# A sparse graph network on one core: gathered rows in a ring, VectorE's order written out, the stages of a group moved closer

## The chip, the cores and the metric

The kernel runs on one core of one Trainium2 chip. Its time is the device time of one execution in microseconds; less is better. The core has five engines with an instruction queue each: TensorE (PE; its weight loads are listed apart as PEld), VectorE (DVE), ScalarE (ACT), GpSimd (POOL) and SyncE (SP, which only starts transfers here). DMA engines move the data; a transfer is started from the queue of SP, ScalarE or GpSimd.

## The reference

Four layers work on 3327 nodes with 256 values each. Layers 0, 2 and 3 are the same block of attention and feed-forward with their own weights, layer 1 is an averaging layer. A node attends only to its neighbours in `adj` (0.24% of all pairs, and itself):

```python
def block(x, adj, w_qkv, w_proj, b_proj, w1, b1, w2, b2, g1, be1, g2, be2):    # 8 heads of 32
    q, k, v = split(layer_norm(x, g1, be1) @ w_qkv)
    scores = jnp.where(adj != 0, einsum('nhd,mhd->hnm', q, k) * SCALE, -inf)
    out = einsum('hnm,mhd->nhd', softmax(scores), v).reshape(n, DIM)
    x = x + out @ w_proj + b_proj
    return x + gelu(layer_norm(x, g2, be2) @ w1 + b1) @ w2 + b2                # 256 -> 1024 -> 256

def averaging(x, adj, Wt, bt, Wa, ba, Wp, bp, gamma, beta):
    h = x @ Wt.T + bt                                                          # 64 values
    s = leaky_relu(h @ Wa.T + ba)                                              # one score a node
    tf = softmax(where(adj > 0, s, NEG), axis=1) @ h @ Wp.T + bp
    return layer_norm(x + tf) * gamma + beta

x = block(x, adj, ...); x = averaging(x, adj, ...); x = block(x, adj, ...); x = block(x, adj, ...)
```

(Abridged: `split` takes the three parts of each row apart.)

## The kernel before

Nodes are handled in 26 tiles of 128 (NP = 3328). The program has five stages, one after the other: adjacency, block 0, averaging, block 1, block 2. The adjacency stage loads the matrix, finds each node's neighbours and sorts the nodes by how many they have; from then on tile 0 holds the nodes with most neighbours. `ROOM[t]` is the number of neighbours, without the node itself, that tile t has places for:

```python
ROOM = [24, 14, 12, 12, 11, 11, 10, 10, 9, 9, 9, 9, 8, 8, 8, 7, 7, 7, 7, 6, 6, 6, 5, 5, 4, 4]
```

They add up to 228; with each node's own row 254 a block.

A block goes through its tiles in the order of `GROUPS` (from few neighbours to many), in groups of one to four tiles. For a tile, `scores` (from line 552) does the following.

- GpSimd starts one indirect DMA for each neighbour place (`gather`, line 546): 128 rows of keys and values, 512 numbers each, into a buffer `unit` of four such places. Ten buffers go round. The node's own row (`own`: key, value, query, x) comes by an indirect DMA (block 0) or from SP's queue (lines 564, 566).
- ScalarE copies x out of `own` (line 568, blocks 0 and 1) and the query into a PSUM bank `qs` (line 571; two banks go round; it also holds the tile's scores).
- VectorE multiplies keys by the query and adds up each head (`dot`: lines 576 and 577), once for `own` and once for each unit of four rows; then it adds the mask (591), takes the maximum (593) and subtracts it (595). ScalarE takes the exponential (596).

`weighed` (from line 599) is done one step after a tile's `scores`: VectorE adds up the exponentials (605), divides (606, 607), multiplies values by weights (610, again once for `own` and once for each unit) and adds: unit upon unit (622, 626), then a unit's four rows in two steps (630), then onto `own`'s part in `o` (631).

When all tiles of a group have their `o`, `project` transposes them (658), copies the transposes (659, ScalarE) and multiplies by the projection's weights (664), after a small matmul that puts the bias into PSUM (`bias`, line 189). The remaining stages of a group are put into a list `later` with the step at which they are to be issued, and `run` issues what is due after each tile: stage 0 is `feed_forward` (VectorE adds the projection onto x at 671, ScalarE sums the squares at 214, VectorE works out the norm in lines 215 to 218, then `turned` normalizes and transposes at 251 to 262, then matmuls f1 at 685, Gelu on ScalarE at 688, matmuls f2 at 695); stage 1 is `end` (the second addition at 671, and what the next layer needs: `finish` of `into_averages` or `into_keys`); stage 2 is the scatter of the results. Stage 0 is due one step after the projection (two for groups of more than two tiles), stage 1 `max(2, len(group))` steps after stage 0.

The order on each engine is not the program's: a scheduler places the instructions of all engines, and VectorE's too, by their dependencies, so that two tiles' work can be mixed. Only the end of the adjacency stage has VectorE's order fixed (`manual_schedule`, line 367). Between a block and the next stage there is a full exchange: the rows that the next layer gathers must have been scattered.

The averaging stage reads a table `between` (its narrow half as `parts`, in two loads at lines 861 to 869), runs `checks` and a column sum (`cps`, `cws`), and then goes through chunks of four tiles: `sums` transposes slices of the stored adjacency on load, into buffers of the same pool as the gathered rows (`units`), and multiplies; a second part makes the averages and block 1's keys.

A dense network stands behind the sparse one, and runs only where the sparse one finds that a node has too many neighbours; in these runs it isn't executed.

## Time and profile before

| | us |
|---|---|
| device time, median of 3 runs | 2089.86 |
| lowest, highest | 2078.97, 2097.79 |
| the profiled execution, its own time | 2096.42 |
| its span in the profile | 2094.6 |
| adjacency / block 0 / averaging / block 1 / block 2 | to 306 / 848 / 1066 / 1604 / the end |

The mean clock granted to TensorE was 0.77 of full speed in the profiled execution. All other times in this document are of such an execution unless they are called a median.

How the profile is read: a row names a line of the kernel, an engine, an operation, the tile written, the tile read, and their shapes, with the number of instructions behind an x; behind the bar the busy time of the group in microseconds, the mean of one in nanoseconds, and the engine's idle time just ahead of them with what ended it. A view by stretches gives each engine's busy time (overlaps of an engine's own instructions counted once) between two moments. A view of waits gives, for an engine and a line, what it waited for: the total in microseconds, how many times, and the longest. A timeline lists single instructions with their start and their duration in microseconds.

### The profile page before, as it was taken

How to read it: one execution, taken by the hardware profiler on the slowest of the kernel's cores; microseconds unless marked ns; L12 is line 12 of the kernel's file. 1: busy time of each engine (PE TensorE's matmuls, PEld its weight loads, DVE VectorE, ACT ScalarE, POOL GpSimd, SP SyncE). 2: the span in 40 equal slices, each digit the busy share in tenths (PEclk: the TensorE clock that was granted, in tenths of full speed). 3: DMA queues.
4: the chain of work that ended last, by engine and by line, in shares of the span. 5: the costliest groups of instructions: out<-in, count | busy, mean ns of one | idle time of the engine just before them, and what ended most of it. 6: DMA issues, size and time to landing. Idle time of an engine off the chain costs nothing. (4 is left out here: it accounts for less than half of the span.)

```text
span 2094.6 us, 17222 instructions
## 1 busy us (share of the span) xinstructions
PE 1263.4 (60%) x4806; PEld 812.1 (39%) x4806; DVE 1342.0 (64%) x3407; ACT 684.9 (33%) x1420; POOL 1001.0 (48%) x946
## 2 busy tenths in 40 slices
PE   3244411556755579699934688567695277655676
PEld 1122200344424337577512454343473154323445
DVE  3567635577776785165636789776732679976871
ACT  3555501233321224122322444334343133322232
POOL 3768757555555531101156645555203666565521
PEclk8667655677767769799976888798798587767778
DMA  8878827555555550858486656656215665565520
GB/s 191 330 300 326 284 79 213 160 163 154 170 148 175 147 131 23 198 154 230 160 284 205 216 166 209 220 178 193 61 56 201 210 186 176 176 190 160 152 65 20
DMA packets 169409, 369.73 MB, mean 177 GB/s; under 512 B 78821, under 2 KB 90291, under 8 KB 165976
## 3 DMA queue, kind: packets, MB, share of 16 engines
q0 software_dynamic: 68624, 222.01, 35.4%
q1 hardware_dynamic: 85689, 112.44, 17.1%
q10 hardware_dynamic: 14990, 34.08, 5.0%
q8 instruction: 40, 0.66, 0.1%
q14 instruction: 66, 0.54, 0.1%
HBM read 279.77 MB, written 77.59 MB: 171 GB/s over the span
## 5 line engine op out<-in xcount | busy, mean ns | idle before, releaser
L546 POOL DMA_INDIRECT unit<-kv,ids x684 | 667.2, 975 | 434.7 <-issue 189.1
L685 PE MATMUL f<-hT,w 128*128 128x256 f32 (+3 forms) x960 | 342.1, 517 | 58.6 <-ACT gT L688 23.2
L256 PE MATMUL tr<-ident,xh 128*128 128x128 f32 x312 | 80.6, 384 | 442.7 <-ACT xh L251 395.6
L695 PE MATMUL f<-w,gT 128*128 128x256 f32 x1248 | 306.4, 399 | 17.9 <-ACT gT L688 14.3
L685 PEld LDWEIGHTS f<-hT,w 128*128 128x128 f32 x960 | 190.4, 219 | 202.6 <-issue 106.0
L695 PEld LDWEIGHTS f<-w,gT 128*128 128x128 f32 x1248 | 238.3, 197 | 68.7 <-ACT gT L688 18.3
L256 PEld LDWEIGHTS tr<-ident,xh 128*128 128x128 f32 x312 | 41.7, 179 | 483.3 <-ACT xh L251 414.8
L576 DVE TENSOR_TENSOR unit<-unit,qs 128x1024 f32<-128x1024 f32 (+3 forms) x198 | 211.7, 1069 | 26.4 <-DMA unit<-kv,ids 15.0
L577 DVE TENSOR_REDUCE qs<-unit 128x32 f32<-128x1024 f32 (+3 forms) x198 | 212.7, 1074 | 4.8 <-DVE qs L607 1.7
L610 DVE TENSOR_TENSOR unit<-unit,qs 128x1024 f32<-128x1024 f32 (+3 forms) x198 | 210.0, 1065 | 0.0
L315 POOL TENSOR_TENSOR m<-a,place 128x3328 f16<-128x3328 fp8e4 x26 | 159.4, 6132 | 78.7 <-ACT a L313 78.6
L688 ACT ACTIVATE gT<-f,b 128x256 f32<-128x256 f32 (+3 forms) x240 | 124.8, 536 | 212.5 <-PE f L685 106.6
L538 PE MATMUL kvps<-wqkv,hT 128*128 128x512 f32 x312 | 171.9, 677 | 29.5 <-ACT hT L262 22.5
L326 DVE MAX8 found<-m 128x8 f16<-128x416 f16 x208 | 111.5, 579 | 39.7 <-POOL m L315 33.1
L664 PE MATMUL proj<-wproj,oT 128*128 128x256 f32 x312 | 109.3, 489 | 42.7 <-ACT oT L659 22.8
L576 DVE TENSOR_TENSOR own<-own,qs 128x256 f32<-128x256 f32 x78 | 32.3, 415 | 141.5 <-ACT qs L571 124.2
L658 PE MATMUL otr<-ident,o 128*128 128x128 f32 x156 | 25.5, 289 | 142.4 <-DVE qs L577 87.4
L990 POOL DMA_INDIRECT sorted<-st,to x26 | 24.8, 955 | 178.7 <-ACT st L542 147.1
L538 PEld LDWEIGHTS kvps<-wqkv,hT 128*128 128x128 f32 x312 | 63.2, 213 | 86.7 <-issue 37.7
L313 ACT ACTIVATE a<-a 128x3328 fp8e4<-128x3328 int32 x26 | 77.3, 2973 | 51.6 <-DMA kv<-st 29.0
L251 ACT ACTIVATE xh<-x,shift,rstd 128x256 f32<-128x256 f32 x104 | 58.4, 594 | 104.5 <-DVE shift L218 80.9
L664 PEld LDWEIGHTS proj<-wproj,oT 128*128 128x128 f32 x312 | 66.9, 235 | 65.6 <-ACT oT L659 28.4
(193 smaller groups left out, 1881.4 us busy)
## 6 DMA issues: line engine op xcount, KB each, us to landing
a<-in_adj SPq DMA_DIRECT2D x25, 1663.5 KB
kv<-st ACTq DMA_DIRECT2D x52, 512.0 KB
own<-sorted SPq DMA_DIRECT2D x26, 512.0 KB
unit<-kv,ids POOLq DMA_INDIRECT x684
adj<-a SPq DMA_DIRECT2D x26, 416.0 KB
own<-qkv SPq DMA_DIRECT2D x26, 384.0 KB
own<-own SPq DMA_DIRECT2D x26, 384.0 KB
w<-in_L_gnn_w SPq DMA_DIRECT2D x6, 1024.0 KB
```

The lines of the kernel that those rows point to most:

```text
L256: nc.tensor.transpose(ps[k][:, ts(q, P)], t[:, ts(k, P)], self.ident)
L315: nc.gpsimd.tensor_mul(m.rearrange("p (s e) -> p s e", e=SEG), a8.rearrange("p (s e) -> p s e", e=SEG), place.unsqueeze(1).to_broadcast([P ...
L326: nc.vector.max(found[:, i, s, :], m[:, ts(s, SEG)])
L538: nc.tensor.matmul(kv, hT[:, k, ts(q, P)], w[:, k, DIM : 3 * DIM], start=k == 0, stop=k == KC - 1)
L546: g = self.nc.gpsimd.indirect_dma_start(out=out, out_offset=None, in_=table, in_offset=bass.IndirectOffsetOnAxis(ap=self.ids[:, t, j : j + ...
L576: nc.vector.tensor_mul(k, k, query.unsqueeze(1).to_broadcast([P, n, DIM]))
L577: nc.vector.tensor_reduce(s[:, ds(at, n), :].rearrange("p j h -> p (j h)"), k.rearrange("p j (h d) -> p j h d", d=HD), AX.X, ALU.add,)
L610: nc.vector.tensor_mul(to.rearrange("p j (h d) -> p j h d", d=HD), v.rearrange("p j (h d) -> p j h d", d=HD), s[:, ds(at, n), :].unsqueeze ...
L664: nc.tensor.matmul(y, oT[:, k, ts(q, P)], wpj[:, k, :], start=False, stop=k == KC - 1)
L685: nc.tensor.matmul(y[:, :w], w1[:, k, ts(f, P)], hT[:, k, :w], start=k == 0, stop=k == KC - 1)
L688: nc.scalar.activation(gT[-1][:, f % 2, :w], y[:, :w], AF.Gelu_apprx_tanh, bias=b1[:, f : f + 1])
L695: nc.tensor.matmul(y, gT[f // 2][:, f % 2, ts(q, P)], w2[:, f, :], start=False, stop=f == FC - 1)
```

## The change

The buffers of four rows are replaced by one ring of 46 places of 512 numbers (`RING`, `take`). A tile takes ROOM + 2 places that lie side by side: its neighbours, and two for its own row, whose key and value then come right behind the neighbours'. So multiplications run over up to six rows at once (`PIECE`, `pieces`), the weighting over up to nine (`WEIGHED`), own row included, and the additions fold the tile's rows in halves.

`fetch` is taken out of `scores`: it starts the own row's and the neighbours' transfers and copies the query, and is called one step ahead, right after `weighed`. x comes by a transfer on SP's queue (block 0: from the ring; block 1: from `sorted`) instead of a copy on ScalarE.

VectorE's instructions in a block keep the order in which the program writes them (`manual_schedule` around the loop); the other engines are scheduled as before. The written order of a step is: `scores` of a tile, the norms and what follows them for groups whose squares are ready (`between`), `weighed` of the tile before, then what `run` has due: additions, squares on ScalarE, scatters. For this `norm` is cut in two (`squares` and `norm`), and `feed_forward` is entered with the squares made. Stage 0 is due one step after the projection, and the second addition `BEHIND` steps after the feed-forward: 2, 2, 3, 3 for groups of one to four tiles. `finish` of `into_averages` hands back its VectorE work (`rest`) to be issued a step later.

The last groups are cut smaller: (6, 5, 4), (3, 2), (1,), (0,) become (6, 5), (4, 3), (2,), (1,), (0,). The last group's feed-forward is put ahead of the other stages that are still due at the end.

A PSUM bank that holds two tiles' results takes both biases in one matmul (`Halves`, `bias`). Gelu results are packed closer into their buffers (`gT`). In the averaging, `parts` is loaded in six pieces in place of two, `checks` and the column sums come after the first chunk's `sums`, and the buffers are places of the ring, each kind by turns.

Of the removed lines only single ones are shown; the longer stretches stand in the kernel above.

```diff
...
+RING = 46
+PIECE = 6
+WEIGHED = 9
...
-    (25, 24), (23, 22), (21, 20, 19), (18, 17, 16, 15), (14, 13, 12, 11), (10, 9, 8, 7), (6, 5, 4), (3, 2), (1,), (0,),
+    (25, 24), (23, 22), (21, 20, 19), (18, 17, 16, 15), (14, 13, 12, 11), (10, 9, 8, 7), (6, 5), (4, 3), (2,), (1,), (0,),
 ]
+BEHIND = (0, 2, 2, 3, 3)
...
+class Halves(list):
+    def __init__(self, banks, n):
+        super().__init__(banks[q // 2][:, ds(q % 2 * DIM, DIM)] for q in range(n))
+        self.banks = banks
+    def bank(self, q):
+        return self.banks[q // 2], min(2, len(self) - q)
+    def ends(self, q):
+        return q % 2 == 1 or q == len(self) - 1
...
-        self.nc.tensor.matmul(y, self.ones3, self.biases[:, i, :], start=True, stop=False)
+    def bias(self, ys, q, i):
+        if q % 2 == 0:
+            bank, n = ys.bank(q)
+            self.nc.tensor.matmul(
+                bank[:, : n * DIM], self.ones3, self.biases[:, i, :].unsqueeze(1).to_broadcast([3, n, DIM]),
+                start=True, stop=False,
+            )
...
             nc.scalar.activation(xh, t, AF.Square, bias=m[:, i : i + 1], accum_out=v[:, i : i + 1])
+        return m, v
+    def norm(self, pool, n, m, v):
+        nc = self.nc
         nc.vector.tensor_scalar(v[:, :n], v[:, :n], 1.0 / DIM, EPS, ALU.mult, ALU.add)
         y = self.root(pool, v, n)
...
+    def take(self, n):
+        if self.at + n > RING:
+            self.at = 0
+        at = self.at
+        self.at += n
+        return self.ring[:, at : at + n, :]
...
-    def scores(self, pool, pp, layer, t, held):
+    def fetch(self, pp, layer, t, held):
         nc = self.nc
         J = ROOM[t]
-        own = pool.tile([P, 4 * DIM], F32, tag="own", name="own", bufs=3)
+        rows = self.take(J + 2)
+        own = rows[:, J:, :].rearrange("p a b -> p (a b)")
         if layer == 0:
             nc.gpsimd.indirect_dma_start(
                 out=own, out_offset=None, in_=self.kv[0][:],
                 in_offset=bass.IndirectOffsetOnAxis(ap=self.row[t], axis=0),
             )
+            nc.sync.dma_start(out=self.x[t], in_=own[:, 3 * DIM :])
         elif layer == 1:
-            self.after(nc.sync.dma_start(out=own, in_=self.sorted[ts(t, P), :]), self.turning)
+            for to, at in ((own[:, : 3 * DIM], self.sorted[ts(t, P), : 3 * DIM]), (self.x[t], self.sorted[ts(t, P), 3 * DIM :])):
+                self.after(nc.sync.dma_start(out=to, in_=at), self.turning)
         else:
             nc.sync.dma_start(out=own[:, : 3 * DIM], in_=self.own[t])
...
+        for j in range(J):
+            self.gather(rows[:, j, :], self.places[layer], t, j, held)
         bank = pp.tile([P, CW], F32, tag="qs", name="qs", bufs=2)
         query = bank[:, :DIM]
         nc.scalar.copy(query, own[:, 2 * DIM : 3 * DIM])
+        return rows, bank
+    def scores(self, pool, t, rows, bank):
+        nc = self.nc
+        J = ROOM[t]
+        n = J + 1
+        query = bank[:, :DIM]
         s = bank[:, ds(DIM, (SLOTS + 1) * HEADS)].rearrange("p (j h) -> p j h", h=HEADS)
...
+        for lo, w in self.pieces(n, PIECE):
+            k = rows[:, ds(lo, w), :DIM]
+            nc.vector.tensor_mul(k, k, query.unsqueeze(1).to_broadcast([P, w, DIM]))
             nc.vector.tensor_reduce(
-                s[:, ds(at, n), :].rearrange("p j h -> p (j h)"), k.rearrange("p j (h d) -> p j h d", d=HD), AX.X,
+                s[:, ds(lo, w), :].rearrange("p j h -> p (j h)"), k.rearrange("p j (h d) -> p j h d", d=HD), AX.X,
                 ALU.add,
             )
...
         away = self.away[:, t, :J].unsqueeze(2).to_broadcast([P, J, HEADS])
-        nc.vector.tensor_add(s[:, ds(1, J), :], s[:, ds(1, J), :], away)
+        nc.vector.tensor_add(s[:, :J, :], s[:, :J, :], away)
         top = pool.tile([P, HEADS], F32, tag="top", name="top", bufs=3)
...
+        nc.vector.tensor_reduce(top, s[:, :n, :].rearrange("p j h -> p h j"), AX.X, ALU.max)
+        nc.vector.tensor_sub(s[:, :n, :], s[:, :n, :], top.unsqueeze(1).to_broadcast([P, n, HEADS]))
+        nc.scalar.activation(s[:, :n, :], s[:, :n, :], AF.Exp)
+        return rows, s
+    @staticmethod
+    def pieces(n, most):
+        count = -(-n // most)
+        at = 0
+        for k in range(count):
+            w = (n - at) // (count - k)
+            yield at, w
+            at += w
+    def weighed(self, pool, t, rows, s):
+        nc = self.nc
+        n = ROOM[t] + 1
         total = pool.tile([P, HEADS], F32, tag="total", name="total", bufs=3)
-        nc.vector.tensor_reduce(total, s[:, : J + 1, :].rearrange("p j h -> p h j"), AX.X, ALU.add)
+        nc.vector.tensor_reduce(total, s[:, :n, :].rearrange("p j h -> p h j"), AX.X, ALU.add)
         nc.vector.reciprocal(total, total)
...
+        nc.vector.tensor_mul(s[:, :n, :], s[:, :n, :], total.unsqueeze(1).to_broadcast([P, n, HEADS]))
+        for lo, w in self.pieces(n, WEIGHED):
+            v = rows[:, ds(lo, w), DIM:].rearrange("p j (h d) -> p j h d", d=HD)
+            nc.vector.tensor_mul(v, v, s[:, ds(lo, w), :].unsqueeze(3).to_broadcast([P, w, HEADS, HD]))
         o = pool.tile([P, DIM], F32, tag="o", name="o", bufs=5)
...
+        v = rows[:, :, DIM:]
         while n > 1:
...
+            half = -(-n // 2)
+            to = v[:, : n - half, :] if n > 2 else o.unsqueeze(1)
+            nc.vector.tensor_add(to, v[:, : n - half, :], v[:, half:n, :])
+            n = half
         return o
...
                     for k in range(KC):
-                        nc.tensor.matmul(y, oT[:, k, ts(q, P)], wpj[:, k, :], start=False, stop=k == KC - 1)
+                        nc.tensor.matmul(
+                            y, oT[:, k, ts(q, P)], wpj[:, k, :], start=False, stop=k == KC - 1 and ys.ends(q)
+                        )
                 return ys
...
-            def feed_forward(group, ys):
+            def squares(group, ys):
+                return self.squares(pool, [self.x[t] for t in group], add(group, ys))
+            def feed_forward(group, sums):
                 w = len(group) * P
-                hT = self.turned(pool, pp, [self.x[t] for t in group], g, b, sums=add(group, ys))
+                hT = self.turned(pool, pp, [self.x[t] for t in group], g, b, sums=sums)
                 gT = []
+                each = 2 * CW // w
                 for f in range(FC):
...
+                    if f % each == 0:
+                        room = pool.tile([P, 2 * CW], F32, tag="gT", name="gT", bufs=4)
+                        gT += [room[:, ds(k * w, w)] for k in range(each)]
...
-            later = []
+            later, middle = [], []
+            def add_later(at, stage, group, what):
+                later.append((at, stage, group, what))
+                later.sort(key=lambda x: (x[0], -x[1]))
+            def forward(at, group, sums):
+                add_later(at + BEHIND[len(group)], 1, group, feed_forward(group, sums))
+                if ahead and group == GROUPS[-1]:
+                    ahead()
+            def follow(at, group, sums):
+                after, rest = finish(group, sums)
+                if rest:
+                    add_later(at + 1, 2, group, rest)
+                add_later(at + 1 + (len(group) > 2 or rest is not None), 3, group, after)
             def run(now):
                 while later and (now is None or later[0][0] <= now):
-                    at, stage, group, ys = later.pop(0)
+                    at, stage, group, what = later.pop(0)
                     if stage == 0:
...
+                        middle.append((forward, at, group, squares(group, what)))
                     elif stage == 1:
-                        later.append((at + 1 + (len(group) > 2), 2, group, end(group, ys)))
+                        if not finish:
+                            add(group, what)
+                            add_later(at + 1 + (len(group) > 2), 3, group, None)
+                        elif normed:
+                            middle.append((follow, at, group, squares(group, what)))
+                        else:
+                            add(group, what)
+                            middle.append((follow, at, group, None))
+                    elif stage == 2:
+                        what()
                     else:
...
+                        scatter(group, what)
+                    if now is None:
+                        between()
+            def between():
+                while middle:
+                    f, *rest = middle.pop(0)
+                    f(*rest)
+            tiles = iter([t for group in GROUPS for t in group])
+            def fetch():
+                t = next(tiles, None)
+                return t is not None and self.fetch(pp, layer, t, held)
+            with tc.manual_schedule(engines={nc.vector.engine}):
+                waiting, step, outs = None, 0, []
+                got = fetch()
+                for group in [*GROUPS, ()]:
+                    for t in group or (None,):
+                        now = t is not None and (group, t, *self.scores(pool, t, *got))
+                        between()
+                        if t is None:
+                            run(step)
+                        if waiting:
+                            done, *rest = waiting
+                            outs.append(attended(*rest))
+                        got = fetch()
+                        if waiting and len(outs) == len(done):
+                            ys, outs = project(done, outs), []
+                            if t is not None:
+                                add_later(step + 1, 0, done, ys)
+                        waiting = now
+                        if begin and step == 2:
+                            begin()
+                        if t is not None:
+                            run(step)
+                        step += 1
+                middle.append((forward, step, done, squares(done, ys)))
+                middle.sort(key=lambda x: x[0] is not forward)
+                between()
+                run(None)
...
+            for lo, hi in ((0, 3), (3, 8), (8, NT // 2)):
+                for n in range(2):
...
+            turn, place = cycle(range(0, 20, 4)), cycle(range(20, 44, 4))
...
-                    at = self.units.tile([P, NT // 2, HALF], BF, tag="unit", name="at")
+                    at = self.ring[:, ds(next(turn), 4), :].rearrange("p a b -> p (a b)").bitcast(BF)[:, : NT // 2 * HALF]
+                    at = at.rearrange("p (g i) -> p g i", i=HALF)
...
+            self.checks(wp, pp, adj)
...
         self.held = []
-        with tc.tile_pool(name="units", bufs=UNITS) as self.units:
+        with tc.tile_pool(name="gathered", bufs=1) as pool:
+            self.ring, self.at = pool.tile([P, RING, 2 * DIM], F32, name="ring"), 0
             self.block(0, got[0], self.into_averages(*args(1, "Wt bt Wa")), lambda: fetch(2, 2))
```

`checks` and the column sums (`cps`, `cws`) move down unchanged. `into_keys` returns `True` as its fourth value (its `finish` is entered with squares), `into_averages` `False`.

## Prediction

> **What bounds the kernel now.** I read the page first (busy shares, chain), then the windows by stage, the waits of VectorE and of GpSimd, and last the timeline of VectorE alone.
>
> ```profile
> PE 1263.4 (60%) x4806; PEld 812.1 (39%) x4806; DVE 1342.0 (64%) x3407; ACT 684.9 (33%) x1420; POOL 1001.0 (48%) x946
> ```
>
> No engine is full; VectorE (DVE) is the fullest. The windows cut the run at its stages: block 0 (306 to 848), averaging (848 to 1066), block 1 (1066 to 1604), block 2 (1604 to the end). Each block is cut again where the last tile's attention sum `o` is done:
>
> ```profile
> core 0: us, PE busy (x) PEld busy (x) DVE busy (x) ACT busy (x) POOL busy (x), PEclk, DMA share, GB/s
> 311.00:805.00 494.00, 274.44 (x939) 177.02 (x940) 351.28 (x765) 140.34 (x339) 259.11 (x266) 0.71 0.54 156
> 805.00:848.00 43.00, 36.80 (x213) 30.87 (x212) 13.22 (x67) 18.17 (x61) 10.09 (x11) 0.98 0.32 96
> 848.00:1066.00 218.00, 194.70 (x1101) 134.85 (x1101) 106.21 (x414) 57.46 (x110) 27.86 (x31) 0.92 0.67 189
> 1077.00:1529.00 452.00, 299.38 (x957) 181.75 (x958) 342.89 (x753) 166.37 (x363) 234.95 (x239) 0.79 0.58 182
> 1529.00:1605.00 76.00, 68.30 (x301) 47.94 (x299) 13.62 (x81) 40.68 (x107) 10.36 (x11) 1.00 0.33 118
> 1611.00:2048.00 437.00, 251.59 (x825) 157.98 (x826) 339.51 (x718) 119.43 (x247) 243.65 (x248) 0.73 0.55 165
> 2048.00:2094.00 46.00, 31.22 (x172) 26.13 (x170) 4.62 (x27) 12.81 (x35) 5.73 (x6) 0.87 0.07 23
> ```
>
> See two things. In the long stretches VectorE works 351, 343 and 340 us of 494, 452 and 437, so it stands idle for 143 + 109 + 97 = 349 us. The tails (43, 76, 46) and the averaging (195 of 218) belong to TensorE. So the blocks last as long as VectorE's work plus its waits. What it waits for:
>
> ```profile
> DVE own L576 <- ACT qs L571: 124.2, 22, 24.4
> DVE x L671 <- PE f L695: 73.4, 12, 12.5
> DVE total L605 <- ACT qs L596: 31.3, 17, 9.0
> DVE unit L576 <- DMA unit<-kv,ids: 15.0, 4, 7.7
> POOL unit L546 <- DVE o L631: 64.4, 11, 8.2
> ```
>
> The largest is the query copy on ScalarE (124 us, 22 times, 5.6 us each). For gathered rows VectorE waits 15 us in all, while GpSimd waits for VectorE to free buffers: gathers run ahead and are not the bound.
>
> **What the change does to VectorE's work.** Two rows of the page's kind give the price of an instruction by size.
>
> ```profile
> L630 DVE TENSOR_TENSOR unit<-unit 128x256 f32<-128x256 f32 x78 | 32.5, 417 | 1.8 <-DVE qs L591 1.2 <-DVE qs L595 0.5
> L622 DVE TENSOR_TENSOR unit<-unit 128x1024 f32<-128x1024 f32 x66 | 80.2, 1216 | 0.0
> ```
>
> (1216 - 417) / 768 = 1.04 ns an element, so 1.04 x 256 = 266 of the 417 are data and about 150 ns are fixed. Elements stay the same (254 rows a block, 228 additions). Instructions do not: multiplications, reductions and weighings were 92 each per block (66 units and 26 own rows); by the list ROOM they become 54, 54 and 39. Additions were 22 + 18 + 52 + 26 = 118 and become 94. That is 153 fewer a block, 153 x 0.15 = 22.8 us of durations. The eleventh group adds back 8 norm instructions of 0.16 (twice in block 1; with some 10 of the averaging's in block 0): 3.0, 2.6, 1.3 us.
>
> But durations are not occupancy. The timeline:
>
> ```profile
> 1688.45 1.21 DVE L576 TENSOR_TENSOR unit<-unit,qs 128x1024 f32<-128x1024 f32 x1
> 1689.58 0.42 DVE L631 TENSOR_TENSOR o<-o,unit 128x256 f32<-128x256 f32 x1
> 1689.92 1.22 DVE L577 TENSOR_REDUCE qs<-unit 128x32 f32<-128x1024 f32 x1
> ...
> 1046.65 0.16 DVE L200 TENSOR_TENSOR nwt<-ve,rstd 128x2 f32<-128x2 f32 x1
> 1046.85 0.16 DVE L201 SCALAR_TENSOR_TENSOR nwt<-nwt,rstd 128x2 f32<-128x2 f32 x1
> 1047.04 0.16 DVE L202 SCALAR_TENSOR_TENSOR rstd<-nwt,rstd 128x2 f32<-128x2 f32 x1
> ```
>
> Above, the scheduler has woven two tiles together: the next instruction needs nothing of the one before and starts 0.08 us before its end. Below, each needs the one before, and starts 0.04 after its end. A dependent step so costs 0.12 more. In block 2's stretch the 718 durations add up to 393.6 us against 339.5 busy: nearly everything overlaps now. In the built order of before only 8 to 20 instructions a block read what the one just ahead wrote; in the changed kernel, whose VectorE follows the program, it is 447, 461 and 405 (multiply then reduce, mask then maximum then subtract, sum then reciprocal then scale, each addition on the last). So for blocks 0, 1, 2: durations 427, 413, 399 now; less 22.8 and plus the extra group 407, 392, 377; dependent steps x 0.04 add 18, 18, 16; the other 253, 236, 194 overlap by 0.08 and take off 20, 19, 16. Occupancy becomes 405, 391, 377 against 367, 357, 344 busy today: **+38, +34, +33 = +105 us.** Written out and taken alone, VectorE's new order is a loss. Bounds: if dependent steps overlapped like the others, occupancy would be some 50 us a block less (-45 in place of +105); if each lost a further 0.04, 52 us more in all.
>
> The row for the fixed part: 150 ns by duration, 70 when overlapped, 190 when dependent. The Trainium skill (Perfetto Trace Analysis, Optimizing Scalar/DVE Operations) puts it at about 60 ns a VectorE instruction, the write-acknowledgement half being hidden by the next one; by that rule 459 instructions save 28 us and nothing is added, and the sum below would be near 1811. The same section says that where VectorE is not saturated but makes others wait, instructions are better broken up, which speaks against pieces of six rows.
>
> Pieces of six wait for six gathers, up to 2 x 1.25 us more than of four, where gathers are late: at a block's start and at tile 0, whose 26 ring rows take the places of tiles 3 and 2. I allow 4 us a block inside the waits below.
>
> **Waits.** Of the 349 us, query copies are 124. Waits with no known releaser (issue, remote), added over the longer rows, are 115. Landings (rows, own) are 27. The rest is exp, the norm's squares, the projection and the averaging's matmul, 97. The new order moves each of that last kind half a step or a step behind its cause (weighing after the next tile's scores, norm after the scores, addition one step after the projection; a step is about 14 us): 97 goes to 8. The query copy is issued right after the previous tile's weighing frees its bank; the additions that follow hide its 0.38 us unless ScalarE stands at a Gelu that waits for TensorE: 124 to 40. ScalarE also loses 52 copies of x (0.40 us each, and 123 us of waiting for own rows ahead of them). They become 52 transfers on SP's queue, before a use more than a step later: nothing, and 2 to 3 us per group if late. Unknown waits: half stay, 60. Landings stay, 27. **349 to 135, -214.** Shorter distances: a group of four takes 16 us (f1) and 15 (f2) at the clock of 0.9, some 36 from its norm, against about 33 left by three steps: a wait of 3 us, nine times, inside the 40 and 60.
>
> **Tails.** Smaller last groups leave less TensorE work after the last `o`: block 1 has 68 us busy there; two feed-forwards of 7.5, the projections of the last tiles and a chain of some 15 make about 50 to 55, so -22. Blocks 0 and 2: two feed-forwards of 7.5 and the same chain, -8 and -9. **-39** (0 to -60). Splitting a group costs some 3 us a block of TensorE, inside this; 66 fewer bias matmuls of 0.29, but wider, are put at zero beside idle TensorE time (up to 6 us a block if that cover went).
>
> **Averaging.** TensorE's first sum starts at 868.7, 6 us after `parts` is first read at 862.8; tables in slices and sums ahead of the checks: **-4** (0 to -8). Ring places there are as many as units before: nothing, a few us if a transpose waits.
>
> Sum against the profiled run's own 2096.4: +105 - 214 - 39 - 4 = -152, so 1944. The median of the three runs (2078.97 to 2097.79) is 2089.86, 0.3% lower: 1938, say **1940**.
>
> **Rivals.**
> (a) The waits only move, and it gets slower. Mechanism: the query copy stands in ScalarE's single queue behind Gelus, its bank is free only when the previous tile is weighed, and VectorE now has no second tile to turn to. For it: 22 such waits today, though the scheduler could fill in. Against it: the built ScalarE order has at most about four Gelus between the freeing and the copy. If the idle 349 stays: 1944 + 214 = 2158, less 0.3% 2150. It decides from 287 us on, 3.7 a tile against 4.5 today and 1.7 in my sum.
> (b) Dependent steps cost nothing: 1944 - 150 = 1794, some 1790. For it only that dependent pairs of long instructions are rare in this trace; against it the gaps of 0.04.
> (c) Waits go as I say only by half (349 to 240) and the tails stay: 1944 + 105 + 39 = 2088: no change.
> That VectorE's order is not as written is excluded by the built order.
>
> **Numbers.** The forecast (idle 70 to 210) has 0.65 and lies at 1875 to 2020. (b) or nearly so 0.13; (c) and its neighbourhood 0.13, of which about half still lies over 1% below; (a) 0.09. So faster by over 1% (about what a measurement here can tell) 0.84, same 0.07, slower 0.09. The range takes in half of (b)'s effect and the upper part of the forecast with unchanged tails: 1850 to 2050.
>
> **What would show it.** VectorE's busy time (overlaps taken out) barely changes or falls while gaps of 0.04 us appear by the hundred: step right. Query-copy waits under 50 us, exp waits gone: right; over 124, (a). The long stretches at 420 to 440 us in all blocks. I am wrong if they stay at 494, 452 and 437, or if instructions in a dependent chain still overlap.

## The result, and the profile after

The changed kernel takes 2163.89 us in the median of four runs (2158.80 to 2169.54), the kernel before 2084.41 of four: 1.038 times as long, 95% interval 1.031 to 1.045. It is slower, where 1940 us and faster was forecast; 2163.89 lies above the range. The profiled execution took 2162.23 us, with a span of 2160.5 against 2094.6.

The page's row of engines, and the stretches cut as before (blocks 0, 1, 2 up to the last `o`, the stretch behind each, the averaging third):

```profile
PE 1249.2 (58%) x4836; PEld 832.5 (39%) x4836; DVE 1421.5 (66%) x2992; ACT 689.3 (32%) x1416; POOL 1008.2 (47%) x946
```

```profile
core 0: us, PE busy (x) PEld busy (x) DVE busy (x) ACT busy (x) POOL busy (x), PEclk, DMA share, GB/s
311.00:821.00 510.00, 272.69 (x1023) 190.34 (x1023) 380.81 (x632) 143.88 (x326) 270.15 (x275) 0.74 0.53 160
821.00:864.00 43.00, 27.46 (x138) 21.93 (x138) 11.49 (x60) 14.10 (x45) 4.69 (x5) 0.74 0.70 160
864.00:1087.00 223.00, 198.93 (x1101) 134.53 (x1101) 106.86 (x414) 57.63 (x110) 28.11 (x31) 0.92 0.59 182
1100.00:1615.00 515.00, 332.63 (x1108) 213.52 (x1108) 373.06 (x637) 180.75 (x400) 236.90 (x239) 0.78 0.53 167
1615.00:1663.00 48.00, 37.11 (x159) 26.74 (x159) 9.77 (x62) 22.48 (x61) 4.80 (x6) 0.86 0.38 131
1671.00:2121.00 450.00, 248.73 (x898) 170.22 (x899) 363.39 (x574) 129.05 (x268) 244.97 (x245) 0.76 0.53 154
2121.00:2160.00 39.00, 21.22 (x108) 17.58 (x108) 4.31 (x26) 9.76 (x27) 2.88 (x3) 0.72 0.04 13
```

VectorE has 415 instructions fewer and is busy 80 us longer. Two of the three short stretches shrank as forecast (76 to 48, 46 to 39), the third did not (43 both times), and the long ones grew. What VectorE and GpSimd wait for now, from the view of waits (us in total, times, longest):

```profile
DVE ring L624 <- DMA ring<-kv,ids: 83.7, 8, 33.3
DVE x L705 <- PE f L734: 69.3, 11, 17.3
DVE ring L624 <- ACT qs L610: 59.6, 9, 16.9
DVE x L705 <- remote: 42.0, 6, 15.7
DVE x L705 <- PE proj L696: 35.7, 10, 10.2
...
POOL ring L583 <- ACT qs L610: 204.7, 31, 18.8
```

The wait for the exponential is gone, that for the query copy is halved, and the additions' (`L705`) has taken their place. "Remote" and "issue" stand for a wait whose end the profile ties to no instruction. GpSimd's row is new: its gathers now wait for query copies.

So that runs can be compared, the span is cut into five parts that add up to it: 306 us of adjacency; in the blocks, from the first gather (block 0: from 306) to the last `o`, VectorE's occupancy (busy time and gaps under 0.15 us) and its waits (gaps above that); the starts (from a block's first gather, or from 306, to VectorE's first instruction); and the rest (tails and averaging). All are added up over the trace's single instructions:

| run, chip | occupancy | waits | starts | rest | span |
|---|---|---|---|---|---|
| before | 1038.6 | 346.1 | 11.3 | 392.9 | 2094.6 |
| changed | 1164.7 | 313.7 | 22.4 | 353.7 | 2160.5 |

Occupancy +126, waits -32, starts +11, rest -39: +66 us.

### The profile page after: what moved, and what is told of

The parts are those of the page before. It is cut to its first block, busy times and chain, and to the rows that moved or that the text cites. A ratio compares the mean times of both kernels' runs of the same rounds, so it can differ in the third digit from the quotient of the medians.

```text
span 2160.5 us, 17039 instructions
## 1 busy us (share of the span) xinstructions
PE 1249.2 (58%) x4836; PEld 832.5 (39%) x4836; DVE 1421.5 (66%) x2992; ACT 689.3 (32%) x1416; POOL 1008.2 (47%) x946
## 5 line engine op out<-in xcount | busy, mean ns | idle before, releaser
L583 POOL DMA_INDIRECT ring<-kv,ids x684 | 671.8, 982 | 530.8 <-issue 207.3
L624 DVE TENSOR_TENSOR ring<-ring,qs 128x1280 f32<-128x1280 f32 (+3 forms) x162 | 227.8, 1406 | 158.3 <-DMA ring<-kv,ids 83.7
L734 PE MATMUL f<-w,gT 128*128 128x256 f32 x1248 | 287.2, 387 | 10.8 <-ACT gT L727 6.8
L724 PEld LDWEIGHTS f<-hT,w 128*128 128x128 f32 x1056 | 206.8, 223 | 150.0 <-issue 83.0
L625 DVE TENSOR_REDUCE qs<-ring 128x40 f32<-128x1280 f32 (+3 forms) x162 | 229.3, 1416 | 19.4 <-issue 7.1
L657 DVE TENSOR_TENSOR ring<-ring,qs 128x1280 f32<-128x1280 f32 (+4 forms) x117 | 217.7, 1888 | 6.1 <-DVE qs L654 2.4
L663 DVE TENSOR_TENSOR ring<-ring 128x768 f32<-128x768 f32 (+6 forms) x204 | 194.0, 951 | 7.1
L1063 POOL DMA_INDIRECT sorted<-ring,to x26 | 25.5, 979 | 178.9 <-ACT ring L571 146.4
L705 DVE SCALAR_TENSOR_TENSOR x<-f,x 128x256 f32<-128x256 f32 x78 | 29.8, 420 | 111.4 <-PE f L734 69.3
L691 ACT COPY oT<-otr 128x256 f32<-128x256 f32 (+3 forms) x66 | 24.5, 413 | 239.2 <-remote 124.0
```

What stands on the lines that cost most here:

```text
L583: g = self.nc.gpsimd.indirect_dma_start(out=out, out_offset=None, in_=table, in_offset=bass.IndirectOffsetOnAxis(ap=self.ids[:, t, j : j + ...
L624: nc.vector.tensor_mul(k, k, query.unsqueeze(1).to_broadcast([P, w, DIM]))
L625: nc.vector.tensor_reduce(s[:, ds(lo, w), :].rearrange("p j h -> p (j h)"), k.rearrange("p j (h d) -> p j h d", d=HD), AX.X, ALU.add,)
L657: nc.vector.tensor_mul(v, v, s[:, ds(lo, w), :].unsqueeze(3).to_broadcast([P, w, HEADS, HD]))
L663: nc.vector.tensor_add(to, v[:, : n - half, :], v[:, half:n, :])
L724: nc.tensor.matmul(y[:, :w], w1[:, k, ts(f, P)], hT[:, k, :w], start=k == 0, stop=k == KC - 1)
```

## The experiments

Eighteen runs fell on four chips, and chips turned out to be of two kinds: the kernel before takes 2076 us on chip 7 and 2070 on chip 15, but 1909 on chips 12 and 14. The forecast's chip, with 2084, is of the first kind. Ratios are to the kernel before on the same chip, with the 95% interval.

| run | chip | us | ratio | occupancy | waits | starts | rest |
|---|---|---|---|---|---|---|---|
| query_in_place | 7 | 2068.46 | 1.000 (0.995 to 1.005) | 1155.5 | 216.4 | 21.9 | 353.9 |
| longer_distance | 7 | 2131.30 | 1.027 (1.018 to 1.037) | 1162.1 | 292.2 | 21.8 | 350.5 |
| scheduler_order | 7 | 2075.25 | 1.000 (0.995 to 1.004) | 1013.7 | 346.2 | 22.7 | 399.2 |
| gathers_in_turn | 7 | 2235.75 | 1.075 (1.064 to 1.086) | 1164.2 | 391.2 | 22.7 | 355.1 |
| changed_again | 15 | 2135.04 | 1.030 (1.023 to 1.037) | 1162.4 | 285.7 | 22.6 | 354.9 |
| query_in_place_2 | 15 | 2087.29 | 1.005 (1.000 to 1.010) | 1151.2 | 241.7 | 21.6 | 352.2 |
| woven_2 | 15 | 2107.31 | 1.014 (1.006 to 1.023) | 1066.6 | 393.0 | 21.2 | 325.2 |
| changed_3 | 12 | 1992.90 | 1.043 (1.038 to 1.049) | 1166.2 | 144.5 | 22.3 | 353.5 |
| woven | 12 | 1905.62 | 0.998 (0.996 to 0.999) | 1062.0 | 192.9 | 21.8 | 327.4 |
| woven_in_place | 12 | 1913.73 | 1.002 (0.999 to 1.005) | 1060.9 | 199.4 | 20.6 | 325.1 |
| woven_in_place_2 | 12 | 1912.43 | 1.001 (0.999 to 1.004) | 1058.6 | 197.2 | 21.9 | 327.8 |
| in_place_scheduler | 12 | 1956.97 | 1.023 (1.019 to 1.028) | 1006.0 | 218.4 | 23.2 | 402.4 |
| before_in_place | 12 | 1904.73 | 0.997 (0.994 to 1.000) | 1026.3 | 166.3 | 8.6 | 399.1 |
| old_distances | 14 | 1997.88 | 1.047 (1.044 to 1.050) | 1164.5 | 144.9 | 22.7 | 357.8 |
| in_place_old | 14 | 1995.77 | 1.045 (1.041 to 1.048) | 1155.4 | 154.6 | 20.9 | 355.9 |
| in_place_old_woven | 14 | 1930.18 | 1.010 (1.006 to 1.013) | 1059.3 | 212.1 | 21.1 | 333.0 |
| before_in_place_2 | 14 | 1907.78 | 0.999 (0.996 to 1.001) | 1028.8 | 165.7 | 9.1 | 397.2 |

**The query read in place.** VectorE reads it from the ring, and the copy on ScalarE falls away.

```diff
-        query = bank[:, :DIM]
+        query = rows[:, J + 1, :DIM]
```

> The changed kernel (2164 us) with VectorE reading the query from its place in the ring; the copy on ScalarE and its PSUM space fall away. Theory A (with VectorE's order fixed, the copy for the next tile stands in ScalarE's queue behind a feed-forward's Gelus and VectorE has nothing else to do): the waits of the first multiplication for the copy, 60 us, go, and so do the 205 us that gathers wait for copies; 2090 to 2120 us. Rival B (VectorE is bound by its own dependent steps, waits only change places): 2155 to 2170. Rival C (two operands from SBUF make the multiplication slower): the mean of a multiplication of 1280 elements leaves 1.49 us upwards, and the time is above 2164.

2068 us, below Theory A's range: the copy's rows are gone, and with them 97 us of waits against the changed kernel on the forecast's chip. That compares two chips. The repetition beside the changed kernel on chip 15 takes off 44 us of waits and 0.025 of the ratio, between its two expectations:

> The changed kernel with the query read in place (no copy). On the chip with standstills it was 1.000 times the kernel before. Theory A (the copy's wait is the engines' queues, whichever chip): 0.03 to 0.05 under the changed kernel's ratio on this chip too. Rival B (the copy is late only through standstills): within 0.015 of the changed kernel's ratio where there are none.

Rival C is out, by the row of the multiplication in the first of them:

```profile
L623 DVE TENSOR_TENSOR ring<-ring 128x1280 f32<-128x1280 f32 (+3 forms) x162 | 227.8, 1406 | 111.4 <-DMA ring<-kv,ids 102.7
```

The changed kernel's row has the same 227.8 us and 1406 ns, and its multiplications of 1280 elements take 1486 ns against 1485 here.

**The second addition later.** `BEHIND` becomes (0, 3, 3, 4, 4).

> The changed kernel with the second addition one step later after the feed-forward (3, 3, 4, 4 steps for groups of 1 to 4). Theory A (the shortened distances are too short: VectorE waits 94 us in the long stretches at the second addition, against 21 before the change): these waits fall under 35 us and the time to 2095 to 2130. Rival B (the wait only moves to the query copy behind the same Gelus): 2150 to 2170, the waits of the first multiplication growing by what the addition's lose.

2131 us. The waits at the second addition fall from 94 us to 1 in the blocks, and those at the first rise from 43 to 130. Of the waits for a known releaser, in this run:

```profile
DVE x L705 <- PE proj L696: 99.4, 15, 23.7
```

The wait moved, but not to the copy, and 2131 lies 1 us above Theory A's range: neither expectation has it right.

**The scheduler's order on VectorE.** The `manual_schedule` around the loop is left out.

> The changed kernel without the fixed order on VectorE: the scheduler places its instructions as before the change. Theory A (the written order costs twice: about 83 us of overlap between instructions, and waits in which another tile's work could have been done): 2040 to 2090 us, VectorE's busy time in the long stretches back to 340 to 355. Rival B (the ring, larger pieces and shorter distances are what costs): 2130 to 2180 us though the overlaps come back.

2075 us, in Theory A's range, with half of its reason: occupancy falls by 151 us, but the waits, which were to fall too, rise to 346, and the rest to 399. In block 1, from the last `o` to block 2's first gather takes 79.1 us, as before (80.0), though the last groups are cut smaller; in the written order it is 48.1.

**Gathers in turn.** In the changed kernel the scheduler puts single gathers of far tiles ahead of nearer ones, into places that an own row leaves early; they wait for that row's query copy, and the queue with them. Here an ordering hint holds each gather behind the one before.

> The changed kernel with the gathers on GpSimd's queue held to the order in which tiles use them (an ordering hint alone, no wait added). In the changed kernel single gathers for tiles two to five steps ahead stand in the queue before those of nearer tiles and wait for a query copy (205 us on GpSimd). Theory A (those waits lie beside VectorE's work except at the starts of blocks and the largest tiles): within 15 us of 2164. Rival B (late gathers are what VectorE waits for): 2100 to 2135 us, and the waits for transfers of gathered rows, 84 us, fall under 40.

2236 us, outside both; VectorE's waits for gathered rows rise from 84 to 112 us. The hint changes the queue's other entries too: in this run GpSimd waits with a scatter at its head for ScalarE 155.0 us, against 76.6 in the changed kernel. What it shows is that the hint is bad, not what the far gathers cost; that stays open.

**Scores and weighing in turn.** `scores` and `weighed` become generators that yield after each VectorE instruction:

```diff
...
+                while streams:
+                    streams = [x for x in streams if next(x, self) is not self]
+                    turns += 1
+                    if turns == 4:
+                        between()
...
```

> The changed kernel with VectorE's written order changed: the instructions of a tile's scores and of the weighing of the tile before are written in turn, one of each, so that most of them no longer read what the one ahead wrote; the norms come after the fourth turn. Query copy as in the changed kernel. Theory A (dependent steps cost VectorE the overlap of 0.08 us and a gap of 0.04 each, and this is on the path): busy time plus small gaps in the three blocks fall from 1165 us by 80 to 120, and the time to 2045 to 2095 us. Rival B (what VectorE saves it waits for the query copy and the feed-forwards): occupancy falls as much, but the time stays at 2130 to 2170.

> The changed kernel with the scores of a tile and the weighing of the one before written in turn. On the chip without standstills it was 0.9975 times the kernel before, with 1062 us of busy time and small gaps in the three blocks. Theory A (dependent steps are the loss on either chip): 0.03 to 0.05 under the changed kernel's ratio on this chip. Rival B (what they cost is hidden in other waits): within 0.015 of it.

`woven` fell on chip 12, `woven_2` on chip 15. Here the two kinds of chips part, so the changed kernel was run on both.

> The changed kernel once more, for a profile on the same chip as the three beside it. The first eight runs came from two chips: on one the kernel before takes 2076 us, and its engines also stand still for some hundred us with nothing to wait for (rows named issue and remote, on ScalarE, TensorE and VectorE); on the other it takes 1909 and these rows are nearly empty. Theory A (the loss is VectorE's: dependent steps, and a first multiplication and additions that stand behind late work): 1.02 to 1.05 times the kernel before on either chip. Rival B (the standstills hurt a fixed order more, and are the loss): 1.03 to 1.045 where there are standstills, 0.98 to 1.01 where there are none.

> The changed kernel. Theory A (on a chip without standstills VectorE's occupancy is the loss, as old_distances and in_place_old show, 1.045 to 1.047 there): 1.03 to 1.05 times before on such a chip, with waits over 0.15 us in the three blocks of 150 to 200 us; 1.030 to 1.038 on one with standstills, waits 285 to 315. Rival B (the longer distances of old_distances cost time of their own): 1.00 to 1.02 on a chip without standstills.

The changed kernel is slower on both kinds, 1.030 and 1.043 times: Theory A in both expectations (the 144.5 us of waits lie just under its 150 to 200). On chip 12 weaving lowers occupancy by 104 us and the span from 1992.3 to 1910.1: Theory A again (its microseconds were for a chip with the kernel before at 2076), and the ratio falls from 1.043 to 0.998, although the waits rise by 48. On chip 15 weaving lowers occupancy by 96 us, but the waits rise by 107, and 1.030 becomes 1.014, a little more than Rival B of `woven_2` allows and half of what Theory A asks. Why waits differ shows in ScalarE's timeline. The changed kernel on the forecast's chip, in a feed-forward of block 1 (start, duration, operation, and in brackets the idle time ahead and what ended it):

```profile
1461.40 0.69 ACT L727 ACTIVATE gT<-f,b 128x512 f32<-128x512 f32 x1 [1.85 <-issue]
1467.41 0.69 ACT L727 ACTIVATE gT<-f,b 128x512 f32<-128x512 f32 x1 [5.33 <-remote]
1469.54 0.69 ACT L727 ACTIVATE gT<-f,b 128x512 f32<-128x512 f32 x1 [1.44 <-PE f L724]
1470.12 0.38 ACT L610 COPY qs<-ring 128x256 f32<-128x256 f32 x1
```

And on chip 12 the same three Gelus (both runs have one order of instructions on ScalarE and on VectorE):

```profile
1331.82 0.69 ACT L727 ACTIVATE gT<-f,b 128x512 f32<-128x512 f32 x1 [1.90 <-PE f L724]
1334.13 0.69 ACT L727 ACTIVATE gT<-f,b 128x512 f32<-128x512 f32 x1 [1.62 <-PE f L724]
1335.85 0.69 ACT L727 ACTIVATE gT<-f,b 128x512 f32<-128x512 f32 x1 [1.03 <-PE f L724]
```

On chip 12 a Gelu follows each 1.7 to 2.3 us, as matmuls deliver. On the other, the second comes 6 us after the first with a releaser that the profile can't name, and the query copy stands behind it. By the trace, whose matmul ends are modelled, its four matmuls had ended at 1464.1, so 3.3 of the 6 us are ScalarE standing still with its data there, a standstill; the first Gelu, put down to "issue", starts 0.04 us behind its last matmul and isn't late at all. VectorE's timeline meanwhile:

```profile
1453.17 0.43 DVE L663 TENSOR_TENSOR o<-ring 128x256 f32<-128x256 f32 x1
1470.53 1.22 DVE L624 TENSOR_TENSOR ring<-ring,qs 128x1024 f32<-128x1024 f32 x1 [16.94 <-ACT qs L610]
```

and on chip 12, the same instruction:

```profile
1336.84 1.22 DVE L624 TENSOR_TENSOR ring<-ring,qs 128x1024 f32<-128x1024 f32 x1 [4.75 <-ACT qs L610]
```

The wait for this copy is 16.9 us on one chip and 4.8 on the other: the place behind three Gelus costs the smaller part.

Over the whole run ScalarE's idle time put down to "remote" and "issue" is 174 + 134 us in the kernel before on the forecast's chip, 183 + 136 in the changed one, and 0 + 2 (before_in_place) and 0 + 8 (changed_3) on chip 12. These sums are no measure of the standstills: the traces from the slower kind of chip have lost records. The changed kernel's holds 13,421 semaphore events where changed_3, the same program, has 24,387, and a wait whose event is missing can get one of these two names. A count without names takes each Gelu's start against the end of its fourth matmul and of ScalarE's instruction before. It is over 0.3 us late 36 times in the kernel before (104.5 us in all) and 28 times in the changed one (57.9), but 2 and 3 times (0.8 and 1.4) in before_in_place and changed_3. VectorE, too, waits 24 and 26 us in the blocks with no releaser but an earlier instruction of its own, and none of this on chip 12. So the standstills are real, and their full size is not known.

A run of the kernel before on chip 15 (`before_again`) repeated its time (2073.68 us). It was to show whether the query copy's wait is one of 90 to 110 us with standstills. Its trace, of an execution of 2097.81 us, has as many waits in the blocks as the one before (345.1 against 346.1), but this row instead of 124.2:

```profile
DVE own L576 <- ACT qs L571: 87.6, 15, 26.4
```

**Both, and the old distances.** In `woven_in_place` both edits; `in_place_scheduler` is `query_in_place` without the fixed order; `before_in_place` reads the query from `own` in the kernel before.

> The same weaving by hand, and the query read in place. Theory A: the two gains add up, 95 us from the copy and 80 to 120 from the weaving: 1945 to 1990 us. Rival B (with the copy gone the feed-forward and the gathers are next): 2020 to 2065.

> The query read in place, scores and weighing written in turn. Theory A (with standstills two things hold VectorE up in a fixed order, the late copy and the dependent steps, and taking away one alone lets the other show): 0.96 to 0.985 times before on a chip with standstills, 1.00 on one without. Rival B (with standstills the group's chain through ScalarE and TensorE sets the pace whatever VectorE does): 0.995 to 1.015 on a chip with standstills.

> The changed kernel without the fixed order on VectorE, and with the query read in place. Theory A (the copy held VectorE up under either order): the waits of the first multiplication fall from 99 us to under 50, and the time from 2075 to 2000 to 2035 us. Rival B (the scheduler had other work for VectorE in those waits): 2055 to 2080.

> The kernel before with one edit: VectorE reads the query from the own row's buffer, without ScalarE's copy. Theory A (the copy is the largest wait of the kernel before too, 105 us in the long stretches): 1985 to 2025 us against 2076. Rival B (other waits follow at once): 2050 to 2080.

All fell on chip 12. Taken as ratios, only Rival B of `before_in_place` holds, and Theory A of `woven_in_place_2` for a chip without standstills. The gains don't add up: 1.002 with the copy gone, 0.998 with it. Nor does the copy cost the kernel before anything there (0.997). As `woven_in_place_2` fell on chip 12 again, this version was never run with standstills. What the ring costs where VectorE's order is free (1.023) shows in the waits for gathered rows, of `in_place_scheduler`:

```profile
DVE ring L623 <- DMA ring<-kv,ids: 231.7, 43, 31.2
```

and of `before_in_place`:

```profile
DVE unit L575 <- DMA unit<-kv,ids: 62.4, 21, 8.5
```

In the blocks alone, without their starts, it is 180 against 62.

Three of the other four undo the distances (first addition two steps after the projection for groups of three and four, `BEHIND` 4 for four); `before_in_place_2` is `before_in_place` once more:

```diff
-BEHIND = (0, 2, 2, 3, 3)
+BEHIND = (0, 2, 2, 3, 4)
...
-                                add_later(step + 1, 0, done, ys)
+                                add_later(step + 1 + (len(done) > 2), 0, done, ys)
```

> The changed kernel with the distances of before: the first addition two steps after the projection for groups of three and four, the second four steps after the feed-forward for groups of four. Theory A (the distances of large groups cost most of the 94 us that VectorE waits at the second addition): 0.015 to 0.035 under the changed kernel's 1.030 times before. Rival B (the query copy takes over the wait): 1.015 to 1.035.

> The query read in place and the distances of before, both on the changed kernel. Theory A (both waits are of ScalarE's and TensorE's queues, and independent): 0.965 to 0.985 times before, waits over 0.15 us in the three blocks under 190 us in all. Rival B (VectorE's occupancy is next): 0.99 to 1.01.

> As in_place_old, and VectorE's scores and weighing written in turn (about 97 us less of busy time and small gaps). Theory A (occupancy decides once the waits are gone): 0.93 to 0.96 times before. Rival B (the chain of a group through ScalarE and TensorE sets the pace, and what VectorE saves it waits): 0.97 to 1.00.

> The kernel before with the query read in place. On the chip without standstills it was 0.997 times before. Theory A (there the copy was not late; where engines stand still it is, 105 us in the long stretches): 0.95 to 0.98 on a chip where before takes 2070. Rival B (the scheduler fills these waits in either way): 0.99 to 1.005.

All four fell on chip 14, without standstills, and the ratios expected had the other kind in mind: only Rival B of `before_in_place_2` holds as written. On this kind of chip neither the distances (1.047 beside 1.043 on chip 12) nor the copy (1.045) matter, and weaving does (1.010). With standstills the old distances were not tried. No version is more than 0.3% faster than the kernel before, which is not clear of noise.

## Why the prediction was wrong

**Occupancy: right in kind and near in size.** +105 was forecast for whole blocks. It is +120 there (1073.5 to 1193.5), and +126 up to the last `o`. Dependent steps leave a gap: in the whole blocks there are 1363 gaps under 0.15 us of 0.034 us each (the forecast: 1313 of 0.04). Of the independent pairs, 515 overlap where 683 were counted, and they save 42 us for 55; the durations come to 1188 us for 1176. These two make up the difference, and more; the gaps come to 47 us for 52. The profile of the changed kernel shows such a chain:

```profile
1526.18 0.26 DVE L652 TENSOR_REDUCE total<-qs 128x8 f32<-128x104 f32 x1
1526.47 0.20 DVE L653 RECIPROCAL total<-total 128x8 f32<-128x8 f32 x1
1526.71 0.27 DVE L654 TENSOR_TENSOR qs<-qs,total 128x104 f32<-128x104 f32 x1
```

The weaving settles it: the same instructions in another order take 104 us less of VectorE (chip 12). The Trainium skill (Perfetto Trace Analysis, Optimizing Scalar/DVE Operations) gives a VectorE instruction on SBUF a fixed part of about 60 ns; by the forecast's estimate from it VectorE would have been 28 us faster here. For independent neighbours the trace comes near it: some 150 ns less an overlap of 81 leave 70, an estimate. Where the next instruction reads what the last wrote, the overlap is gone, and 0.034 us are added.

**Waits: the step that failed.** "349 to 135, -214" came out as 346 to 314. By the forecast's terms, in us, in the blocks from VectorE's first instruction on:

| what VectorE waits for | forecast: now, then | before | changed | changed_3 (chip 12) |
|---|---|---|---|---|
| query copy | 124, 40 | 100 | 60 | 29 |
| no known releaser | 115, 60 | 118 | 101 | 0 |
| landings | 27, 27 | 15 | 34 | 27 |
| the rest | 97, 8 | 90 | 93 | 89 |
| an earlier instruction of its own | | 24 | 26 | 0 |

"97 goes to 8" missed most, on both kinds of chips. Half a step or a step was to hide what VectorE waits for. The exponential is hidden, the averaging's matmul nearly, but the first addition waits 27 us for the projection, and the second 52 for the feed-forward (9 times, up to 17.3, where 3 us nine times were allowed); both wait 58 us more for no known releaser. On chip 12 it is 30 and 49, and nothing more. A group's chain through TensorE and ScalarE lasts longer than the steps that the distances leave, and another distance alone doesn't help: both additions together wait 136 us in the changed kernel and 131 in `longer_distance`, 79 in changed_3 and 74 in `old_distances`.

The second miss is what the 115 and much of the 124 are made of. On chip 12 the changed kernel has 144.5 us of waits, near the forecast's 135, but by luck: 89 for 8, and nothing for 60. There the kernel before has about 166, if its twin with the query in place may stand for it (0.997 of its time; the kernel before itself has no profile there). So of the 346 us that the profile of before showed, about 180 are waits that only chips with standstills have, and the changed kernel has nearly as many more there itself (313.7 - 144.5 = 169). The forecast read them as waits of the written program: it let the "waits with no known releaser" fall by half, and the query copy's to a third, because the new order puts it early. The copy's wait is 60 us instead of 40, and in the case shown above 12 of its 17 us are not there on chip 12.

Without standstills the change takes 22 of the 166. The averaging's matmul (28 us) is hidden and gathered rows cost 27 for 62, but the two additions wait more (49 and 30 us against 33 and 21 in `before_in_place`), and the query copy, which the twin lacks, has 29.

The four terms add up to 363 and not to 349: 24.4 of the copy's 124 and most of the 12 for `own` stand at the starts of blocks 1 and 2, ahead of the stretches. The 135 doesn't rest on this.

**Tails: -39 forecast, -39 measured with the averaging**, but by luck in the sum and by another cause. Block 1 gave -32 for -22, block 2 -7 for -9, block 0 and the averaging together nothing for -12. The smaller last groups alone leave 79.1 us behind block 1 (`scheduler_order`); it is the written order, with the last group's feed-forward first, that makes it 48.1. The part behind block 0's last `o` takes 266.0 us against 266.4.

**Starts**: 12 us were allowed for pieces of six in the three blocks. VectorE's first multiplication comes 323.6 us into the run against 311.7 in block 0, and 12.5 and 8.5 us behind the first gather against 6.0 and 2.8 in the others: 24. Before, the first multiplication took the own row alone; now it waits for the tile's gathers as well.

**Rivals.** (a) came out, at 2150 for 2164: the query copy behind Gelus, and no second tile to turn to; `query_in_place` takes 0.025 to 0.038 off the ratio with standstills. The number is partly luck, as (a) had 349 us of waits for the 314 measured. Nor is it the whole cause: without standstills taking the copy away gains nothing, as other waits take its place, and the changed kernel is 4.3% slower all the same, by occupancy: woven, it is level with the kernel before. (b) is refuted by the gaps. So on both kinds of chips the added occupancy is there, as forecast, and the waits fall by 32 and 22 us, too little to pay for it. With standstills it is not the only thing that shows: there weaving gains 0.016 and the missing copy 0.025.

## What to carry to other kernels

Writing an engine's order by hand gives up the scheduler's weaving: put independent instructions of two tiles in turn, or count 0.1 us for each dependent step. Before a wait is put on a forecast's account, ask why its releaser was late: where engines stand still for no reason shown, a queue behind them looks like a scheduling fault, and where records are missing, a row without a releaser may be an ordinary wait. Move one wait of a chain, and look for it at the next link before calling it gone.

## What the runs showed of the hardware

The same kernel takes 1909 us on two chips and 2070 to 2084 on the others, with the same durations of instructions (1406 ns for the changed kernel's multiplications on both kinds). What differs is idle time. ScalarE's Gelus start late with their data there, up to 10.6 us in the kernel before, and VectorE waits up to 1.5 us for earlier instructions of its own; of TensorE only rows without a releaser tell. All traces from the slower kind of chip also hold fewer semaphore events (13,421 to 16,817, against 23,765 to 24,449); whether the two have one cause isn't known. The standstills are not seen to be tied to the packets that load instructions: of ScalarE's 68 waits over 1 us for no known releaser in the kernel before, 6 have such a packet in the 2.5 us ahead of their end, no more than the 11% that random moments have. Their cause stays open.

A multiplication whose second operand comes from SBUF in place of PSUM took no longer (227.8 us for 162 either way), so the copy into PSUM bought nothing here.
